# Output parts fetched three ahead of their split, and expert weight rows one per other part, in the stage after cross attention of a decoder layer

## The chip, the cores and the metric

One core of a Trainium2 chip. The metric is the device time of one execution in microseconds, the median over the runs shown; the profile is of one execution. PE is TensorE, DVE VectorE, ACT ScalarE, POOL GpSimd, SP SyncE, which issues most transfers. PEld is the weight load of PE.

## What is computed

A decoder layer on x of 16 x 100 tokens, width 512, fp32, with a context of 16 x 361 rows:

```python
x = layernorm(x + self_attention(x))            # 16 heads of 32, causal
x = layernorm(x + cross_attention(x, ctx))      # 16 query heads of 128, 4 key heads,
                                                # RMS norm on q and k, then o @ Wo (2048 x 512)
x = layernorm(x + ffn(x))                       # router over 8 experts, top 2, silu(x @ We + be),
                                                # weighted sum, projection, RMS norm
```

The 1600 tokens make NT = 13 tiles, twelve of 128 tokens and one of 64.

## The kernel before

Every fp32 product is made of three fast ones. `split` (L133) writes a high part (`dst.h`, a rounded copy, on ACT unless said otherwise, L137) and a low part (`dst.l`, source minus high, on DVE or POOL, L140). `mm3` (L145 to L147) multiplies high by high, high by low and low by high. So L137 and L140 are lines of a helper, and the names of the tiles tell the places apart.

The tile framework orders the instructions of each engine itself, by priority (program order, unless raised) along a timeline that it simulates. `in_turn` and `keep_in_program_order` add an order without a wait. Engines then run their queues in that order; SP too, whose transfers wait in its queue for what they need.

Stages around the change:

- Cross attention runs over 16 batches x 4 groups (b, g) of 4 heads. `x_scores` makes the scores, the row minimum on DVE (L746), the exponential on ACT (L757), the scaling on POOL (L759, tiles p2 and sums2); `x_turn` transposes the probabilities on PE into ptp (L767) and splits them; `x_attend` multiplies by the values, copies av out on ACT (L787) and stores it to the DRAM tiles od (L792).
- The output product (d_ functions) takes od back in parts. A part is (t, g): token tile t and group g, 128 x 4 x 128 values. `parts` lists the 52 of them: for tiles 0 to 9 tile by tile, and for the last TAIL = 3 tiles group by group. `d_load` fetches a part into `of` (2 buffers) and splits it into the pair `ot` (2 buffers), low on DVE for odd parts and on POOL for even ones. `d_part` multiplies it with the rows wo_g: 4 x 3 matmuls of 512 columns onto the tile's accumulator acc. After the fourth group `d_norm` adds x1d (L851, L852), normalises and stores x2d (L854).
- Parts 0 to 3 are written in the program among the last batch's groups (HEAD = 1 per group); the loop at L1320 handles the others, with part i + 1 loaded ahead of part i's product. The framework may run parts of the loop earlier, wherever PE would wait.
- The loop carries more: `d_turn` transposes a finished tile (L933), copies it on ACT (L940), adds a bias on POOL (L941) and stores xbd (L942); `d_logits` makes the router's logits (gb, L952, and lg on DVE, L956); `choose`, `settle` and `slots` work out on DVE, in many small operations (L1049 to L1224), which tokens go to which slot of which expert, ending in is_in (L1224), matmuls on gb (L1239) and idx (L1247). `settle(0, CUT)` needs the logits of tiles 0 to 8; the expert stage's first gathers (`e_gather`, L1263) need idx.
- `load_expert(e)` fetches an expert's four weight rows (128 x 512 each) into `f_e` (the pool stage, 3 buffers, L1312) and splits them into a slot of WH and WL, high on ACT and low on POOL, all four at one place. Experts 1, 2, 4, 5 come at tiles 2, 4, 6, 8; three more (wo_slot) each after the last tile's part of a group, when that group's rows of Wo are no longer needed, since they take their place; the last expert after the loop, two of its rows from the tile `raw`.

The expert stage (e_ functions) and the projection with two norms (f_ functions) follow.

On-chip pools are stacked from both sides. When a pool is opened over the place of a closed one, a tile waits for the tiles that it overlaps (`reuse_waits="tile"`). In a partition, d_in lies at bytes 159936 to 174272 (where attention's kv_in was), and on the other side c_3 (sums2, nm2) at 175232 to 175492, c_1 (nine buffers of p2) from 175520, both of cross attention; later d_3 (tiles x1 of `d_norm`) starts at 176544.

Of the kernel before, what the change touches and what calls it, by code (L numbers as in the profile page):

```python
# [9 lines left out]
FP = mybir.dt.float32  # L10
# [7 lines left out]
B, S, D = 16, 100, 512  # L18
T = B * S
KC = D // 128  # L20
# [4 lines left out]
NKV, HD2 = 4, 128  # L25
GR = NH // NKV
# [36 lines left out]
def tile_decoder_layer(  # L63
# [28 lines left out]
    nc = tc.nc  # L92
# [19 lines left out]
    def pair(p, shape, name, tag=None, bufs=None):  # L112
        k = {} if bufs is None else {"bufs": bufs}
        tag = tag or name
        return Pair(
            p.tile(shape, FR, name=f"{name}_h", tag=f"{tag}_h", **k),
            p.tile(shape, FR, name=f"{name}_l", tag=f"{tag}_l", **k),
        )

    def in_turn(ins, prev):  # L120

        if prev is not None:
            tc.add_manual_dep(
                ins.ins,
                prev.ins.name,
                mybir.DependencyInfo(
                    mybir.DependencyClass.NoSync, mybir.DependencyReason.DATA
                ),
                reason="in_turn",
            )  # L130
        return ins

    def split(dst, src, high=None, low=None):  # L133

        high, low = high or nc.scalar, low or nc.vector
        if high is nc.scalar:
            ins = nc.scalar.copy(dst.h, src)  # L137
        else:
            ins = high.tensor_copy(dst.h, src)  # L139
        low.tensor_tensor(dst.l, src, dst.h.bitcast(FP), ALU.subtract)  # L140
        return ins
# [70 lines left out]
    def kp(w):  # L212
        return w.rearrange("(k p) n -> p k n", p=128)

    NT = len(TT)
# [267 lines left out]
    def split_row(name, k):  # L483
        return split(units[name][:, k], ROW.pop((name, k)), nc.scalar, nc.gpsimd)
# [319 lines left out]
    for h in range(GR):  # L804
        x_scores(0, 0, h)
    order = [(b, g) for b in range(B) for g in range(NKV)]
    OT, X1 = {}, {}

    def d_open():
        kv_l.close()  # L810
        inp["d"] = pool(d_i, "d_in", 2)
# [2 lines left out]
    parts = [(t, g) for t in range(NT - TAIL) for g in range(NKV)]  # L814
    parts += [(t, g) for g in range(NKV) for t in range(NT - TAIL, NT)]

    def d_load(i):
        t, g = parts[i]
        n = TT[t][1]
        p = inp["d"]  # L820
        of = p.tile([128, GR, 128], FP, name=f"of_{t}_{g}", tag="of")
        nc.sync.dma_start(of[:, :, :n], od[t][:, g * GR : (g + 1) * GR, :n])
        OT[t, g] = pair(p, [128, GR, 128], f"ot_{t}_{g}", tag="ot")
        split(OT[t, g][:, :, :n], of[:, :, :n], low=nc.vector if i % 2 else nc.gpsimd)

    def d_part(i, among={}):

# [34 lines left out]
    for i, (b, g) in enumerate(order):  # L862
        if b == B - 1:
            if g == 0:
                d_open()
                d_load(0)
            for j in range(HEAD * g, HEAD * (g + 1)):
                d_load(j + 1)
                d_part(j)
                if parts[j][1] == NKV - 1:  # L870
                    d_norm(parts[j][0])
        if b + 1 < B:
            if g == 0:
                fetch_ctx(b + 1)
                split_ctx(b + 1, 0)
            if g < len(CH):
                kv_project(b + 1, g)
            if g + 1 < len(CH):
                split_ctx(b + 1, g + 1)
        if i + 2 < len(order):  # L880
            x_load(*order[i + 2])
        if b + 1 < B and g == NKV - 1:
            kv_turn(b + 1, 2)
        if b + 1 < B and 1 <= g < NKV - 1:
            kv_turn(b + 1, g - 1)
        nxt = order[i + 1] if i + 1 < len(order) else None
        for what in ("s0", "a-", "t0", "s1", "s2", "t1", "a0", "t2", "s3", "a1"):
            if what[0] == "s":
                if nxt:
                    x_scores(*nxt, int(what[1]))  # L890
            elif what[0] == "t":
                x_turn(b, g, int(what[1]))
            elif what[1] != "-":
                x_attend(b, g, int(what[1]))
            elif i:
                x_attend(*order[i - 1], 2)
        if i % 3 == 2 and 8 <= i < 8 + 3 * NKV * KC:
            w, k = divmod((i - 8) // 3, KC)
            load_row(f"wo_{w}", wo_slot[w], Wo4[w], k)
# [361 lines left out]
    def e_gather(i):  # L1261
        XG[i] = xsp.tile([128, D], FP, name=f"xs_{i}", tag="xs")
        nc.gpsimd.indirect_dma_start(  # L1263
            out=XG[i][:],
            out_offset=None,
            in_=x2d[: CUT * 128] if i < EARLY else x2d[:],
            in_offset=bass.IndirectOffsetOnAxis(ap=SLOT[i][0], axis=0),
        )
# [34 lines left out]

    raw = w1.tile([128, 2, D], FP, name="raw")

    def load_expert(e, last=False):
        for k in range(KC):
            if last and k > 1:
                f = raw[:, k - 2]
            else:  # L1310
                f = stage.tile([128, D], FP, name=f"f_e_{e}_{k}", tag="f")
                tc.keep_in_program_order(nc.sync.dma_start(f, kp(expert_w[e])[:, k]))  # L1312
            split(
                slot_of(e)[:, k],
                f,
                nc.vector if last and k == 1 else nc.scalar,
                nc.vector if last and k else nc.gpsimd,
            )

    for i in range(HEAD * NKV, len(parts)):  # L1320
        t, g = parts[i]
        if i + 1 < len(parts):
            d_load(i + 1)
        among = {}
        if t < NT - TAIL:
            if g == 1:
                d_turn(t - 1)
            if g == 3:
                among = d_logits(t - 1)
            if g == 0 and t in (2, 4, 6, 8):  # L1330
                load_expert(early[t // 2 - 1])
        elif t > NT - TAIL and g == 0:
            if t < NT - 1:
                d_turn(NT - TAIL - 1)
            else:
                among = d_logits(NT - TAIL - 1)
        elif (t, g) == (NT - 1, NKV - 1):
            d_turn(NT - TAIL)
        d_part(i, among)
        if g == NKV - 1:  # L1340
            with tc.high_priority(offset=URGENT if t >= NT - TAIL else 0):
                d_norm(t)
        if t == NT - 1 and g < NKV - 1:
            load_expert(wo_slot[g])
        if (t, g) == (CUT, 0):
            nc.sync.dma_start(raw, kp(expert_w[wo_slot[3]])[:, 2:])
        if t % 3 == 0 and t <= CUT and g == 3:
            choose(t - 3, t)
        if (t, g) == (NT - 1, 0):
            choose(CUT, CUT + 1)  # L1350
        if (t, g) == (CUT, 3):
            settle(0, CUT)
            slots(0, EARLY, CUT)
        if (t, g) == (NT - 1, 1):
            for k in range(4):
                e_gather(k)
    d_i.close()
    ck_l.close()
    load_expert(wo_slot[3], True)
    e_turn(0)  # L1360
    e_turn(1)
    e_product(0, d_logits(NT - TAIL))
# [412 lines left out]
```

## Time and profile before

| | us |
|---|---|
| median of 3 runs | 1432.21 (1428.25 to 1441.84) |
| the profiled execution | 1437.28 |
| its span, first to last instruction | 1435.6 |
| PE busy | 1342.1 (93%) |
| DVE, ACT, POOL busy | 954.1, 746.8, 731.1 |
| mean granted clock of PE | 0.973 of full |

How to read it: a matmul's duration in the profile overlaps the next one's, so pace is read from start to start (0.233 us for 512 columns at full clock). In the slices a digit is the busy share of 1/40 of the span, 35.9 us. In a timeline a line is start, duration, engine, source line, operation, output from input; in brackets how long the engine stood idle before it and what ended that. In a view by stretches the columns are from and to, length, busy time of PE, PEld, DVE, ACT and POOL with the number of instructions, the granted clock, the share of the transfer engines and GB/s.

The output product's first matmul starts at 1002.4 us, cross attention's last od store at about 1087, and the expert stage's first product at 1228.3.

### The profile page before, as it was taken

The numbers are of one execution on the slowest core, as the hardware profiler recorded it, in microseconds if no ns is written. First come the engines' busy times: TensorE is split into PE (matmuls) and PEld (weight loads), VectorE is DVE, ScalarE is ACT, GpSimd is POOL, SyncE is SP. The second block draws the span as 40 slices with busy tenths as digits, with TensorE's granted clock in tenths as the row PEclk, the third lists the DMA queues.
The fourth block names the chain that finished last, engine by engine and source line by source line (L and its number), as shares of the span: only waits on it lengthen the run. The fifth ranks groups of instructions, "written<-read, shape, count | busy, mean of one in ns | idle before, by whom it ended". The sixth has DMA issues, their size and how long they took to land. (4 is left out here: it accounts for less than half of the span.)

```text
span 1435.6 us, 25188 instructions
## 1 busy us (share of the span) xinstructions
PE 1342.1 (93%) x7952; PEld 1107.7 (77%) x7952; DVE 954.1 (66%) x2978; ACT 746.8 (52%) x1872; POOL 731.1 (51%) x854
## 2 busy tenths in 40 slices
PE   8999989999999999999999999999999897988884
PEld 6888878888778888888888888878887674666663
DVE  5766667775567777777777667767555559653698
ACT  4666643444436666566666566656553232332353
POOL 6877653443335555555555455545444445343542
PEclk9999999999999999999999999999999998899898
DMA  5221254555442232323233222223536554666674
GB/s 157 71 92 53 70 161 111 135 92 110 98 103 62 62 74 51 74 63 75 69 75 70 74 68 69 50 65 76 131 81 200 179 165 129 210 227 214 209 239 139
DMA packets 197873, 159.79 MB, mean 111 GB/s; under 512 B 133322, under 2 KB 152878, under 8 KB 197742
## 3 DMA queue, kind: packets, MB, share of 16 engines
q1 hardware_dynamic: 187904, 137.83, 36.2%
q0 software_dynamic: 4576, 14.95, 3.4%
q10 hardware_dynamic: 5262, 5.41, 1.3%
q8 instruction: 65, 1.06, 0.3%
q14 instruction: 66, 0.54, 0.1%
HBM read 107.16 MB, written 50.99 MB: 110 GB/s over the span
## 5 line engine op out<-in xcount | busy, mean ns | idle before, releaser
L759 POOL TENSOR_SCALAR p<-p,sums 100x361 f32<-100x361 f32 x256 | 146.4, 576 | 100.3 <-DVE sums L758 89.3
L746 DVE CUSTOM_DVE_ANT_0 p<-s,nmask 100x361 f32<-100x361 f32 x256 | 132.9, 527 | 64.7 <-PE s L147 56.2
L757 ACT ACTIVATE p<-p,nm 100x361 f32<-100x361 f32 x256 | 153.2, 602 | 39.8 <-DVE nm L746 36.5
L140 DVE TENSOR_TENSOR pT_l<-ptp,pT_h 128x400 fp32r<-128x400 f32 (+1 forms) x192 | 107.4, 567 | 59.3 <-ACT pT_h L137 58.8
L145 PE MATMUL pq<-WH 128*128 128x512 f32 (+2 forms) x272 | 106.5, 392 | 6.2 <-DVE WH L139 5.8
L767 PE MATMUL ptp<-ident,p 100*128 100x100 f32 (+1 forms) x768 | 107.6, 252 | 0.0
L140 POOL TENSOR_TENSOR cT_l<-cf,cT_h 128x512 fp32r<-128x512 f32 (+1 forms) x48 | 54.4, 1134 | 104.2 <-ACT cT_h L137 102.3
L137 ACT CAST pT_h<-ptp 128x400 fp32r<-128x400 f32 (+1 forms) x192 | 91.3, 487 | 30.2 <-PE ptp L767 29.7
L767 PEld LDWEIGHTS ptp<-ident,p 100*128 100x128 f32 (+1 forms) x768 | 95.6, 152 | 13.5 <-POOL p L759 2.3
L146 PE MATMUL pq<-WL,WH 128*128 128x512 f32 (+2 forms) x272 | 104.1, 383 | 0.0
L147 PE MATMUL pq<-WH,WL 128*128 128x512 f32 (+2 forms) x272 | 103.8, 382 | 0.0
L147 PE MATMUL acc<-WH,ot_l 128*128 128x512 f32 (+1 forms) x208 | 87.3, 421 | 8.7 <-DVE ot_l L140 6.9
L145 PE MATMUL acc<-WH,ot_h 128*128 128x512 f32 (+1 forms) x208 | 87.2, 419 | 5.5 <-ACT ot_h L137 5.5
L145 PE MATMUL s<-kT_h,WH 128*100 128x362 f32 x256 | 88.5, 356 | 2.4 <-ACT kT_h L137 2.4
L145 PE MATMUL av<-pT_h,WH 128*128 128x400 f32 (+1 forms) x192 | 77.1, 401 | 11.6 <-ACT pT_h L137 11.1
L146 PE MATMUL acc<-WL,ot_h 128*128 128x512 f32 (+1 forms) x208 | 85.1, 409 | 0.0
L147 PE MATMUL s<-kT_h,WL 128*100 128x362 f32 x256 | 84.5, 330 | 0.0
L146 PE MATMUL s<-kT_l,WH 128*100 128x362 f32 x256 | 83.9, 328 | 0.0
L614 POOL TENSOR_TENSOR qs<-qs,r_q 128x512 f32<-128x512 f32 (+1 forms) x52 | 54.0, 1068 | 58.0 <-DVE r_q L169 47.5
L140 POOL TENSOR_TENSOR WL<-qf,WH 128x400 fp32r<-128x400 f32 x64 | 67.3, 1051 | 31.0 <-ACT WH L137 27.7
L145 PE MATMUL pv<-WH,cT_h 128*128 128x512 f32 (+1 forms) x192 | 80.0, 417 | 1.3 <-DVE WL L140 1.3
L145 PE MATMUL pk<-WH,cT_h 128*128 128x512 f32 (+1 forms) x192 | 77.7, 405 | 0.2
(330 smaller groups left out, 4030.0 us busy)
## 6 DMA issues: line engine op xcount, KB each, us to landing
qf<-qd SPq DMA_DIRECT2D x64, 200.0 KB
of<-od SPq DMA_DIRECT2D x48, 256.0 KB
cf<-in_ctxT SPq DMA_DIRECT2D x16, 722.0 KB
eb<-in_expert_b SPq DMA_DIRECT2D x32, 256.0 KB
ysd<-xs SPq DMA_DIRECT2D x32, 256.0 KB
f_e<-in_expert_w SPq DMA_DIRECT2D x30, 256.0 KB
f_wq<-in_Wq SPq DMA_DIRECT2D x16, 256.0 KB
f_wo<-in_Wo SPq DMA_DIRECT2D x16, 256.0 KB
```

Source lines behind the costliest of these rows:

```text
L137: ins = nc.scalar.copy(dst.h, src)
L140: low.tensor_tensor(dst.l, src, dst.h.bitcast(FP), ALU.subtract)
L145: nc.tensor.matmul(out, a.h, b.h, start=start, stop=False)
L146: nc.tensor.matmul(out, a.h, b.l, start=False, stop=False)
L147: nc.tensor.matmul(out, a.l, b.h, start=False, stop=stop)
L614: nc.gpsimd.tensor_tensor(qr[:, hs, :], qr[:, hs, :], rs[:n, hs].unsqueeze(2).to_broadcast([n, GR, HD2]), ALU.mult,)
L746: nc.vector.tensor_tensor_reduce(out=p, in0=sc[:, :SE], in1=nmask, scale=1.0, scalar=BIG, op0=ALU.add, op1=ALU.min, accum_out=nm,)
L757: nc.scalar.activation(p, p, AF.Exp, bias=nm, scale=-1.0, accum_out=sh)
L759: nc.gpsimd.tensor_scalar(p, p, sh, 1.0, ALU.mult, ALU.mult)
L767: nc.tensor.transpose(pt[:n, h, :], probs[h][:, c0 : c0 + n], ident[:S, :S])
```

## The change

- `d_load` is cut in two. `d_fetch(i)` takes an `of` tile and starts the transfer; `d_load(i)` splits it. In the loop, `d_fetch` runs up to part i + 3 before `d_load(i + 1)`. A pool d_in2 with one buffer of 128 x 4 x 128 (2048 bytes a partition) is opened ahead of the loop; every third part from part 5 on takes its `of` there, the others in d_in. While attention is going on (parts 0 to 4) there is one fetch ahead of one split as before.
- Expert rows are fetched two ahead of the row that is next to be split (`e_fetch`), and split one at a time in `e_rows(i)`: the sixteen rows of experts 1, 2, 4, 5 at parts 6, 8, ... 36, then those of the first three wo_slot experts from part 43 on, with the four rows of an expert on three parts, and the first two rows of the last expert fetched there and split after the loop (`load_last`). Each row's high part is ordered on ACT behind the high part of the output part that was split last.

```diff
-    OT, X1 = {}, {}
+    OT, OF, X1 = {}, {}, {}
+    split_last = [None]
...
+    def d_fetch(i):
+        t, g = parts[i]
+        n = TT[t][1]
+        p = inp["d2"] if "d2" in inp and i % 3 == 2 else inp["d"]
+        OF[i] = of = p.tile([128, GR, 128], FP, name=f"of_{t}_{g}", tag="of")
+        nc.sync.dma_start(of[:, :, :n], od[t][:, g * GR : (g + 1) * GR, :n])
+
     def d_load(i):
         t, g = parts[i]
         n = TT[t][1]
-        p = inp["d"]
-        of = p.tile([128, GR, 128], FP, name=f"of_{t}_{g}", tag="of")
-        nc.sync.dma_start(of[:, :, :n], od[t][:, g * GR : (g + 1) * GR, :n])
-        OT[t, g] = pair(p, [128, GR, 128], f"ot_{t}_{g}", tag="ot")
-        split(OT[t, g][:, :, :n], of[:, :, :n], low=nc.vector if i % 2 else nc.gpsimd)
+        of = OF.pop(i)
+        OT[t, g] = pair(inp["d"], [128, GR, 128], f"ot_{t}_{g}", tag="ot")
+        split_last[0] = split(
+            OT[t, g][:, :, :n], of[:, :, :n], low=nc.vector if i % 2 else nc.gpsimd
+        )
...
                 d_open()
+                d_fetch(0)
                 d_load(0)
             for j in range(HEAD * g, HEAD * (g + 1)):
+                d_fetch(j + 1)
                 d_load(j + 1)
                 d_part(j)
...
-    def load_expert(e, last=False):
+    def load_last(e):
         for k in range(KC):
-            if last and k > 1:
+            if k > 1:
                 f = raw[:, k - 2]
             else:
-                f = stage.tile([128, D], FP, name=f"f_e_{e}_{k}", tag="f")
-                tc.keep_in_program_order(nc.sync.dma_start(f, kp(expert_w[e])[:, k]))
+                f = ROW.pop((f"e_{e}", k))
             split(
                 slot_of(e)[:, k],
                 f,
-                nc.vector if last and k == 1 else nc.scalar,
-                nc.vector if last and k else nc.gpsimd,
-            )
-
+                nc.vector if k == 1 else nc.scalar,
+                nc.vector if k else nc.gpsimd,
+            )
+
+    BY = (NT - TAIL) * NKV
+    erows = [(e, k) for e in early for k in range(KC)]
+    split_at = [HEAD * NKV + 2 + 2 * r for r in range(len(erows))]
+    for g in range(NKV - 1):
+        first = BY + TAIL * (g + 1)
+        erows += [(wo_slot[g], k) for k in range(KC)]
+        split_at += [first + min(k, TAIL - 1) for k in range(KC)]
+    erows += [(wo_slot[-1], k) for k in range(2)]
+    split_at += [len(parts)] * 2
+    rows_in, rows_out = [0], [0]
+
+    def e_rows(i):
+        while rows_out[0] < len(erows) and split_at[rows_out[0]] <= i:
+            e, k = erows[rows_out[0]]
+            in_turn(split_row(f"e_{e}", k), split_last[0])
+            rows_out[0] += 1
+            e_fetch()
+
+    def e_fetch():
+        while rows_in[0] < min(rows_out[0] + 2, len(erows)):
+            e, k = erows[rows_in[0]]
+            fetch_row(f"e_{e}", e, kp(expert_w[e]), k)
+            rows_in[0] += 1
+
+    d2 = ExitStack()
+    inp["d2"] = pool(d2, "d_in2", 1)
+    begun = HEAD * NKV + 1
+    e_fetch()
     for i in range(HEAD * NKV, len(parts)):
         t, g = parts[i]
+        while begun < min(i + 4, len(parts)):
+            d_fetch(begun)
+            begun += 1
         if i + 1 < len(parts):
             d_load(i + 1)
+        e_rows(i)
         among = {}
...
-            if g == 0 and t in (2, 4, 6, 8):
-                load_expert(early[t // 2 - 1])
...
-        if t == NT - 1 and g < NKV - 1:
-            load_expert(wo_slot[g])
...
+    d2.close()
     d_i.close()
     ck_l.close()
-    load_expert(wo_slot[3], True)
+    load_last(wo_slot[3])
```

`fetch_row` and `split_row` are helpers that were there: the first starts a row's transfer into the pool stage, the second splits it, high on ACT and low on POOL.

More of the change, by code (lines that the diff above doesn't have):

```diff
@@ L1315, in load_expert @@
                 f,
-                nc.vector if last and k == 1 else nc.scalar,
-                nc.vector if last and k else nc.gpsimd,
-            )
+                nc.vector if k == 1 else nc.scalar,
+                nc.vector if k else nc.gpsimd,
+            )
+    BY = (NT - TAIL) * NKV
+    erows = [(e, k) for e in early for k in range(KC)]
+    split_at = [HEAD * NKV + 2 + 2 * r for r in range(len(erows))]
+    assert split_at[-1] < BY + TAIL
+    for g in range(NKV - 1):
[20 more added lines that the diff above has]
+    e_fetch()
     for i in range(HEAD * NKV, len(parts)):
         t, g = parts[i]
+        while begun < min(i + 4, len(parts)):
+            d_fetch(begun)
+            begun += 1
         if i + 1 < len(parts):
             d_load(i + 1)
+        e_rows(i)
         among = {}
```

## The prediction

> **What bounds the kernel now.** I read the page's busy shares and slices first, then the busy time in ten-microsecond stretches around the output product that follows cross attention, then the waits there, and last the timelines of PE, ACT, DVE, POOL and SP.
>
> ```profile
> PE 1342.1 (93%) x7952; PEld 1107.7 (77%) x7952; DVE 954.1 (66%) x2978; ACT 746.8 (52%) x1872; POOL 731.1 (51%) x854
> PE   8999989999999999999999999999999897988884
> PEclk9999999999999999999999999999999998899898
> ```
>
> PE is the bound nearly everywhere; its nines break after slice 31 (about 1110 us), which is where the change works. By stretches (PE, PEld, DVE, ACT, POOL busy, then the granted clock):
>
> ```profile
> 1110.00:1120.00 10.00, 5.89 (x27) 3.88 (x25) 5.64 (x16) 2.69 (x5) 3.99 (x4) 1.00 0.59 192
> 1120.00:1130.00 10.00, 9.09 (x38) 7.29 (x39) 7.54 (x23) 2.54 (x6) 6.54 (x5) 0.83 0.52 160
> 1190.00:1200.00 10.00, 6.36 (x22) 3.79 (x21) 9.90 (x25) 2.74 (x5) 4.64 (x4) 0.83 0.53 163
> 1210.00:1220.00 10.00, 4.80 (x47) 3.03 (x46) 9.05 (x24) 2.28 (x6) 5.44 (x5) 0.79 0.33 83
> ```
>
> A hole in PE is followed by a lower clock. The waits of PE from 1095 to 1230 us (us, times, longest) name the splits of the output parts, then routing:
>
> ```profile
> PE acc L147 <- DVE ot_l L140: 5.6, 4, 3.6
> PE acc L145 <- ACT ot_h L137: 5.5, 4, 3.2
> PE gb L1239 <- DVE is_in L1224: 5.0, 2, 4.3
> ```
>
> The largest hole, on the timelines of PE and ACT:
>
> ```profile
> 1119.06 0.50 PE L145 MATMUL acc<-WH,ot_h 128*128 128x512 f32 x1 [3.17 <-ACT ot_h L137]
> 1116.54 0.62 ACT L137 CAST WH<-f_e 128x512 fp32r<-128x512 f32 x1 [6.12 <-DMA f_e<-in_expert_w]
> 1118.39 0.61 ACT L137 CAST ot_h<-of 128x512 fp32r<-128x512 f32 x1
> ```
>
> ACT works in order: two expert-row copies, waiting for their transfers, stood ahead of the part's copy that PE needed. The same view has ACT waiting 28.0 us for of over twelve times; most of that is inside PE's slack.
>
> The end of the stage has another limit, the routing chain on DVE, from the logits of tile 8 (1175.04) to is_in (1216.89): 41.9 us. Its small operations stretch while POOL runs:
>
> ```profile
> 1183.55 3.82 POOL L140 TENSOR_TENSOR WL<-f_e,WH 128x512 fp32r<-128x512 f32 x3
> 1184.83 1.29 DVE L1033 TENSOR_SCALAR i_full<-i_full 128x8 int32<-128x8 int32 x1
> 1187.32 0.19 DVE L1033 TENSOR_SCALAR i_had<-i_had 128x80 int32<-128x80 int32 x1
> ```
>
> The same line takes 1.29 us on 8 columns and 0.19 on 80.
>
> **What the Trainium skill says.** "TensorE: Matmul & The Clock Gate", Part 1, has PE's clock halve after an idle window of about 3.4 us and return after about as much work. The trace agrees in size: from 1120.44 to 1123.60, seven acc matmuls start 0.45 us apart against 0.233 before, 1.5 us lost; but 1.0 us of holes at 1149–1151 was enough for the next such stretch. The same page's section on the array ("Architectural detail") calls ACT and DVE strict FIFO, as the three lines on ACT's queue show. "SBUF — State Buffer", section "SBUF: two separate sides", has DVE and POOL share a port pair as an exclusive lock held for a whole instruction; the two L1033 lines fit. No page gives the transfer's latency for this load; I take the trace's.
>
> **The change part by part.** Counts stay: 52 loads of of, 30 of f_e, the same splits. Only places, one buffer and issue orders are new. I count PE time up to the logits of tile 8, then the chain, then the rest.
>
> *Stalls removed.* PE holes on ot_h or ot_l before 1175: 1.30 (at 1042.6), 1.79 (1086.7), 0.74, 3.17, 0.65, 0.37, 0.59, sum 8.6 us. Slow stretches behind three of them (1089.5, 1120.4, 1151.1): 1.4 + 1.5 + 1.5 = 4.4. Together 13.0. With a fetch issued as soon as a third buffer falls free, about two parts (2 x 12 x 0.233 = 5.6 us) ahead, against a landing of 4.2 us (issue at 1088.46, copy at 1092.63), transfers no longer decide; a row's copy (0.62) and low half (1.29) stand behind a part's copy, one per two parts, not four at once.
>
> *Stalls that stay.* The split pairs still have two buffers: part i+1 may be split only when i-1 has been multiplied, and needs 0.62 + 1.29 + about 0.2 of the 2.8 us; one d_turn addition on POOL (1.29) uses that slack up. DVE can also stand before an ot_l: at 1106.40 it had waited 5.43 us for an x1d load, which no part of the change hurries. SP is in order too, and the earlier fetches stand ahead of x1d loads and xbd stores, waiting for a split. I take 3 us (1 to 6).
>
> *Filler lost.* This is the price I see in the new pool. d_in ends at byte 174272 of a partition; d_in2 takes the next 2048, where cross attention has all its sums2 and nm2 (175232 on) and the first p2 buffer (175520), whose last tenant is the first head of the last group. Part 5, the first in d_in2, can be loaded only after that head's last transpose, and parts 6, 7 and all later ones queue behind it through accumulators and pairs. The trace shows such a wait already: the x1d loads, whose tiles lie on p2 too, go out with the last ptp:
>
> ```profile
> 1076.92 0.53 PE L767 MATMUL ptp<-ident,p 100*105 100x100 f32 x4
> 1077.20 1.37 SPq L851 DMA_DIRECT2D x<-x1d  x3
> ```
>
> Before, some 190 acc matmuls (16 parts) were interleaved with attention by 1077; then only parts 0 to 4 can be. Eleven parts, 31 us of PE work, move behind attention, which finishes earlier by as much if PE stays full without them. From 1057.7 to 1064.2 it did, on attention alone. The drain of the last group can't: last score to last p takes 3.1 us (1063.56 to 1066.7), transposes, splits (0.49 + 0.57) and av another 5, with 3.6 us of PE work in these 8. The load of part 5 starts some 5.8 us after the last score, lands 4.2 later, is copied in 0.6: PE restarts at about 10.5, so 6.9 idle, less what is left of part 4 (0 to 2.8), plus 1.5 of slow clock. I take 6 (2 to 11). Sum to the logits: -13 + 3 + 6 = -4.
>
> *The chain.* The fourth early expert's rows sat on POOL from 1183.6 to 1189.9, inside the chain; five DVE operations took 5.9 us there where 0.2 each is usual. These rows now end with part 36, before part 39's logits. From part 43 on as many wo-slot rows fall in as before, 12. I take -3 (0 to -6).
>
> *After the chain.* PE still had 21 acc matmuls to do behind is_in (1218.0 to 1225.3), twelve at the slow pace (2.4 us lost). If earlier tail parts let them run ahead of the slot matmuls, expert work starts that much sooner; but PE's order may keep them behind. The tail's own holes (1.77, 3.64) and the rest go into the wait for is_in, so they count nothing. I take -1.5 (0 to -5). The expert stage after it is PE-bound (10.00 of 10 busy from 1345 to 1375), so the shift carries through. Loading the last expert's first two rows early gains nothing: their copy at 1223.40 waited for PE.
>
> Sum: -4 - 3 - 1.5 = -8.5 us. The profiled execution took 1437.28 us (span 1435.6 and 1.7 around it), so 1428.8 there; it lies 5.1 above the median of the runs, 1432.2, for which I get 1423.7.
>
> **The rivals.** (a) *All of it pays*: drain covered by part 4 (2), stalls down to 1, chain -6, rest -5: -21, 1411. For: ACT's 28 us of waiting for of; against: two pairs. (b) *It cancels*: stalls 6, drain 11: -0.5, 1432. (c) *Attention starves*: with filler, its groups came 13.4 us apart (copies of av from 1004.44 to 1058.13) for some 4.6 us of PE work each. If that pace is its own and not the filler's, four groups leave 35 us idle less 14 for five parts, 21, with the drain 28, with four slow stretches 34: -13 + 3 + 34 - 4.5 = +19.5, 1452. It is slower than before once this loss passes 14.5 us. Against: the full stretch at 1057.7.
>
> **How the numbers follow.** The forecast has 0.42 (own range 1416 to 1430), (a) 0.36, (b) 0.08, (c) 0.14. One per cent, 14.3 us, is about what a measurement of this kernel can tell from no change. So faster 0.38, within 0.48, slower 0.14. From 1404 to 1444 both unknown prices are covered, and the better part of (c) and a little below (a) is left out.
>
> **What would show it.** Right: no acc wait over 1 us on ACT ot_h after attention; no burst of four WH<-f_e; the last od store some 30 us earlier; of_1_1's load right behind the last ptp, a PE hole of 4 to 7 us there; the stretch from lg to is_in under 40 us. Wrong: parts of tiles 1 to 3 still interleaved with attention (then no loss), or PE holes before the last ptp above 14 us in sum (then c), or the acc waits as long as now.

## Result and profile after: slower by 0.4%

The kernel after took 1439.34 us, median of 20 runs (1432.62 to 1448.74), beside 1433.59 for 20 runs of the kernel before (1428.25 to 1441.84): ratio 1.0038 [1.0023, 1.0053]. A second comparison gave 1.0040 [1.0022, 1.0059]. So it is slower by 5 to 6 us, which is under 1%, but not the 8.5 us gain of the forecast.

The page of the kernel after:

```profile
PE 1341.8 (93%) x7952; PEld 1105.7 (77%) x7952; DVE 951.5 (66%) x2978; ACT 746.9 (52%) x1872; POOL 732.7 (51%) x854
...
PE   8999989999999999999999999999979997789984
...
PEclk9999999999999999999999999999999998789997
```

PE does the same work, with its breaks in other places: one 7 in slice 30 (behind attention), and 77 in slices 34 and 35, the end of the stage. The waits of PE from 1095 to 1230 us, the view in which four holes on ot_h and four on ot_l stood before:

```profile
PE acc L147 <- DVE ot_l L140: 5.6, 1, 5.6
PE pte L1284 <- DMA xs<-x2d,idx: 5.2, 2, 3.1
PE gb L1249 <- DVE is_in L1234: 5.2, 1, 5.2
```

From 1095 us on no part waits for its high half any more; the waits for low halves come to the same sum in one piece. New is the second line: PE waits for the gathers of the expert stage. What the fetch was meant for works, too. The waits of ACT from 1050 to 1175, of before and then of after:

```profile
ACT ot_h L137 <- DMA of<-od: 22.3, 10, 4.3
```

```profile
ACT ot_h L137 <- PE acc L146: 52.6, 32, 3.0
...
ACT ot_h L137 <- DMA of<-od: 4.5, 1, 4.5
```

ACT now waits for PE, not for transfers. The price of d_in2 is there as well: the first load into it goes out behind the last ptp, and PE stops, then works at a lower clock (SP's timeline, then PE's, then ten us by stretches):

```profile
1048.31 0.99 SPq L480 DMA_DIRECT2D f_e<-in_expert_w  x2
1049.40 0.37 SPq L823 DMA_DIRECT2D of<-od  x1
```

```profile
1047.46 0.53 PE L767 MATMUL ptp<-ident,p 100*105 100x100 f32 x4
...
1055.65 0.80 PE L145 MATMUL acc<-WH,ot_h 128*128 128x512 f32 x1 [5.85 <-ACT ot_h L137]
```

```profile
1050.00:1060.00 10.00, 4.35 (x13) 3.47 (x14) 1.62 (x11) 1.57 (x3) 2.47 (x8) 0.66 0.94 193
```

The loss lies further on. A table of the stations from tile 8's logits (lg) to the first expert product, one row for each profiled execution; "chain" is from lg to the end of the second is_in, "rows" the expert rows that POOL splits in it, all of them rows of the late experts, the last column the first product (first ph matmul) less idx:

| kernel | ratio to before [interval] | lg of tile 8 | chain (rows) | is_in to idx | idx | product 0 less idx |
|---|---|---|---|---|---|---|
| before | | 1175.0 | 41.9 (12) | 1.5 | 1218.3 | 10.0 |
| before2 | | 1175.3 | 42.6 (12) | 1.5 | 1219.3 | 10.3 |
| after | 1.0038 [1.0023, 1.0053] | 1170.0 | 42.7 (11) | 5.0 | 1217.6 | 16.2 |
| after2 | 1.0040 [1.0022, 1.0059] | 1172.8 | 40.3 (9) | 4.9 | 1218.0 | 16.3 |
| nolap | 1.0054 [1.0034, 1.0073] | 1170.5 | 40.5 (9) | 4.7 | 1215.8 | 16.5 |
| fe_act | 1.0032 [1.0017, 1.0048] | 1173.8 | 42.7 (11) | 4.0 | 1220.5 | 9.9 |
| nolap_act | 1.0012 [0.9998, 1.0026] | 1170.4 | 42.7 (11) | 5.1 | 1218.2 | 9.3 |
| nolap_act_j | 1.0014 [0.9994, 1.0035] | 1172.2 | 40.2 (9) | 5.0 | 1217.4 | 8.8 |
| early_only | 1.0003 [0.9990, 1.0017] | 1172.9 | 42.6 (12) | 3.9 | 1219.4 | 10.1 |
| nolap_early | 1.0032 [1.0018, 1.0045] | 1168.8 | 42.7 (12) | 3.9 | 1215.4 | 9.6 |
| fetch_only | 1.0146 [1.0123, 1.0168] | 1190.3 | 43.1 (12) | 3.4 | 1236.8 | 9.5 |
| rows_only | 1.0070 [1.0045, 1.0095] | 1176.5 | 40.8 (10) | 5.2 | 1222.4 | 15.7 |
| tail_pool_j | 1.0025 [1.0010, 1.0040] | 1172.6 | 41.8 (11) | 1.2 | 1215.7 | 14.0 |
| no_wl | one run | 1170.2 | 29.3 (0) | 4.0 | 1203.4 | 16.3 |
| dve_low | 0.9986 [0.9967, 1.0005] | 1175.7 | 47.6 (1) | 1.2 | 1224.5 | 9.3 |
| after_dve_low | 0.9990 [0.9973, 1.0008] | 1169.9 | 43.3 (0) | 3.2 | 1216.3 | 9.3 |
| before_dve_low | 0.9993 [0.9978, 1.0008] | 1172.3 | 46.2 (1) | 1.2 | 1219.7 | 8.8 |
| dve_idx_ra | 0.9961 [0.9946, 0.9977] | 1171.4 | 38.3 (1) | 1.2 | 1210.9 | 13.0 |
| before_idx | 0.9978 [0.9962, 0.9994] | 1169.5 | 39.1 (1) | 1.2 | 1209.8 | 11.5 |

The median of the kernel before lay between 1429.33 and 1433.59 us in the comparisons, so kernels are compared by their ratios. In before and before2 product 0 starts at 1228.3 and 1229.5, in after and after2 at 1233.8 and 1234.3: later by 5.2 us in the mean, as much as the time grew.

The delay does not last, though. The fifth product starts at 1253.2 and 1253.1 in before and before2, and at 1252.0 and 1251.2 in after and after2; the ninth at 1268.0 and 1268.1, and at 1267.5 and 1267.6. By then PE has made the delay good. idx is worked out twice, first for eleven products and then for the other 21, and the kernel after falls behind again where the second is needed (DVE's timeline of before2 and then of after):

```profile
1272.04 0.18 DVE L1247 CAST idx<-gb 128x21 int32<-128x21 f32 x1 [0.24 <-PE gb L1239]
```

```profile
1277.09 0.18 DVE L1257 CAST idx<-gb 128x21 int32<-128x21 f32 x1 [0.22 <-PE gb L1249]
```

The thirteenth product starts at 1287.4 and 1286.3 in the two executions of before, and at 1293.9 and 1294.6 in those of after. The second idx needs the logits of the last tiles, and the last of these came at 1244.2 and 1245.5, and at 1252.7 and 1251.9. So the late first product equals the loss in size, but it is not shown to be the way in which the time is lost.

### The profile page after: what moved, and what is told of

It is laid out like the page before. It is cut to its first block, busy times and chain, and to the rows that moved or that the text cites. A ratio compares the mean times of both kernels' runs of the same rounds, so it can differ in the third digit from the quotient of the medians.

```text
span 1437.2 us, 25178 instructions
## 1 busy us (share of the span) xinstructions
PE 1341.8 (93%) x7952; PEld 1105.7 (77%) x7952; DVE 951.5 (66%) x2978; ACT 746.9 (52%) x1872; POOL 732.7 (51%) x854
## 5 line engine op out<-in xcount | busy, mean ns | idle before, releaser
L145 PE MATMUL av<-pT_h,WH 128*128 128x400 f32 (+1 forms) x192 | 77.1, 402 | 10.6 <-ACT pT_h L137 10.3
```

The lines of the kernel that those rows point to most:

```text
L145: nc.tensor.matmul(out, a.h, b.h, start=start, stop=False)
```

## The experiments

**Which readings belong to the kernel** (before2 and after2 are the two kernels unchanged).

> The kernel before, profiled once more, to tell which of its readings belong to the kernel and which to one execution. If the expert stage simply carries its start through to the end, the 5.6 us hole of PE at 1330 (a gather's semaphore) should not come back, the first expert product should stand near 1228 and the span near 1430.5, the median less 1.7. If the hole belongs to the kernel, it is there again within 1 us of its size, the span is near 1435, and the late first product of the kernel after (5.5 us) was paid for by something else.

Span 1429.7 us, product 0 at 1229.5, no hole at 1330. The hole belonged to one execution, and so did most of the 5.1 us by which the profiled execution lay above the median.

> The kernel after once more. If the late rows belong to the kernel, product 0 again follows idx by 15 to 17 us, idx follows the end of is_in by 4 to 5 us, and the logits of tile 8 stand at 1168 to 1174; ratio to the kernel before 1.002 to 1.006. If they belong to one execution, product 0 follows idx by 10 us.

All as expected: idx 4.9 behind is_in, product 0 another 16.3 behind idx.

**Why product 0 is late.** SP's timeline of the kernel after and then of the kernel before (f_e are expert rows, x2d the stores of normalised tiles):

```profile
1200.19 4.84 SPq L480 DMA_DIRECT2D f_e<-in_expert_w  x3
1218.80 0.34 SPq L862 DMA_DIRECT2D x2d<-x  x1
1219.35 0.27 SPq L480 DMA_DIRECT2D f_e<-in_expert_w  x1
...
1220.22 0.42 SPq L862 DMA_DIRECT2D x2d<-x  x1
1220.85 0.88 SPq L480 DMA_DIRECT2D f_e<-in_expert_w  x2
```

```profile
1209.35 2.82 SPq L1312 DMA_DIRECT2D f_e<-in_expert_w  x3
1221.23 0.34 SPq L854 DMA_DIRECT2D x2d<-x  x1
```

In the kernel after the last three fetches come two rows ahead of their split, that is late in the program, and in SP's queue they stand behind a load that waits for idx (L1301) and behind the stores of tiles 10 and 11, which wait for their norms. They go out ten us later than before, and their copies follow at 1224.97 and 1229.53 on ACT and at 1233.28 on DVE; product 0 starts at 1233.84. The rows are not all that product 0 had to wait for. Right ahead of it PE stands at the transposes of tile 12, which need that tile's norm, and DVE's copy of the last row stands in its queue behind the same norm (PE's timeline of the kernel after):

```profile
1233.23 0.66 PE L943 MATMUL ptx<-ident,x 64*128 64x64 f32 x4 [3.66 <-DVE hit L1064]
1233.84 1.20 PE L145 MATMUL ph<-WH,xsT_h 128*128 x2
```

This wait of 3.66 us stands ahead of product 0 in the five executions in which it comes some 16 us behind idx (after, after2, nolap, rows_only and no_wl), and in no other. Whether the rows, the norm or PE's order held product 0 was not separated.

A product picks its expert's rows by a register, so it waits for every row of WH and WL. Three edits test this. fe_act issues the last three rows from ACT's queue; nolap keeps d_in2 away from attention; nolap_act does both (of fe_act only the choice of the queue is shown):

```diff
-            fetch_row(f"e_{e}", e, kp(expert_w[e]), k)
+            q = nc.scalar if len(erows) - rows_in[0] <= 3 else nc.sync
+            fetch_row(f"e_{e}", e, kp(expert_w[e]), k, q)
...
```

```diff
-        p = inp["d2"] if "d2" in inp and i % 3 == 2 else inp["d"]
+        p = inp["d2"] if "d2" in inp and i % 3 == 2 and i >= 20 else inp["d"]
```

> The kernel after, with the last three weight rows (one of expert 0, two of expert 6) issued from ACT's queue, so that they no longer stand behind the stores of x2d on SP. Theory B (late rows): their copies stand before 1223, product 0 starts at 1227 to 1229 instead of 1233.8, time 4 to 6 us under the kernel after, about 1434. Theory A (filler lost, rows without effect): product 0 is held by the gathers and the slow clock, at 1231 or later, time within 1.5 us of the kernel after. Theory C (the expert stage absorbs its start): product 0 earlier by 5, time within 1 us of the kernel after.

> The kernel after, with d_in2 used from part 20 on only: the parts before part 20 keep the two buffers of d_in, which don't overlap attention's tiles, so parts can fill attention again. Theory A (filler was lost): some 180 acc matmuls interleaved with attention again, no 5.9 us hole behind the last ptp and no slow stretch there, less whatever stalls come back for want of a third buffer in parts 5 to 19 (up to 4 us); logits of tile 8 at 1165 to 1168 instead of 1170.0, time 3 to 5 us under the kernel after, 1434 to 1436. Theory B (the late rows of the last expert alone set the start of the expert products): these hang on the norm of tile 10, which moves with the logits, so the gain carries through here too; the delay between the last slot matmul and product 0 stays at 16 us. Theory C (the expert stage absorbs its start): logits earlier, time within 1 us of the kernel after, 1439.

> Both edits together: d_in2 from part 20 on, the last three rows from ACT's queue. If both losses are real and separate (A and B): product 0 at 1221 to 1225, time 8 to 10 us under the kernel after, 1429 to 1431, that is 2 to 4 us faster than the kernel before. If only one of them counts, 1434. Under theory C 1439.

The delay behaved as theory B says: 9.9 and 9.3 us behind idx with the edit, 16.5 without it. The time did so for one pair: nolap_act is 4.2 per mille (6 us) under nolap, though only 2.6 to 2.8 per mille (4 us) under the kernel after, where both theories together had 8 to 10. fe_act is only 0.6 to 0.8 per mille under the kernel after, far from the 4 to 6 us expected. Its fetches moved into another queue that works in order (ACT's timeline of fe_act):

```profile
1214.28 0.34 ACTq L480 DMA_DIRECT2D f_e<-in_expert_w  x1
1218.53 0.20 ACT L157 ACTIVATE a_ln<-v_ln 128x1 f32<-128x1 f32 x1 [5.09 <-DVE v_ln L179]
1218.64 0.60 ACT L137 CAST WH<-f_e 128x512 fp32r<-128x512 f32 x1
1218.77 0.34 ACTq L480 DMA_DIRECT2D f_e<-in_expert_w  x1
```

The last row now waits behind a norm's logarithm. In this execution idx, too, came 2.5 to 2.9 us later than in the two of the kernel after. Yet product 0 came 3.4 to 3.9 us earlier than there, and the time gained only 1 us, so an earlier product 0 is not an equal gain. The second idx came at 1276.0 and the thirteenth product at 1294.0, about as in the kernel after.

Theory A failed: nolap's logits were no earlier than those of the kernel after, and its time no better. Over the pairs the overlap has no steady sign (nolap over after by 1.5 per mille, nolap_act under fe_act by 2.0, nolap_early over early_only by 2.9).

early_only is the cleanest test: the kernel after with the late rows as in the kernel before (the lists of late rows go, `load_expert` comes back).

```diff
+        if t == NT - 1 and g < NKV - 1:
+            load_expert(wo_slot[g])
...
-    load_last(wo_slot[3])
+    load_expert(wo_slot[3], True)
```

> The kernel after, with the rows of the last four experts fetched and split as in the kernel before (four at a time behind the last tile's parts), the first sixteen rows still one per other part, and the fetch three ahead. Theory B (late rows): the last fetches stand ahead of bat's load and the x2d stores on SP again, product 0 follows idx by 10 us instead of 16.2, time 4 to 6 us under the kernel after, 0.999 to 1.001 of the kernel before. Rival (the delay comes from the gathers or from the slow clock): product 0 at idx plus 14 or more, time within 1.5 us of the kernel after.

```profile
1203.36 8.62 SPq L1322 DMA_DIRECT2D f_e<-in_expert_w  x6
1220.53 0.34 SPq L862 DMA_DIRECT2D x2d<-x  x1
```

All fetches ahead of the first x2d store again, product 0 10.1 us behind idx, and the time equal to that of the kernel before, 3.5 per mille (5 us) under the kernel after. So in this pair the late rows are all of the loss, and the rest of the change comes to nothing. The other pairs with and without late rows go the same way by other amounts: fe_act lies 0.6 to 0.8 per mille under the kernel after, nolap_act 4.2 and nolap_early 2.2 under nolap; for early_only and nolap_act the intervals are apart. That the late rows cost time is shown, somewhere from 1 to 6 us. By which way is not: in early_only's profiled execution, 2.8 us above the median of its runs, the second idx (1275.8) and the thirteenth product (1292.5), too, came 4 to 6 us later than in before and before2. Why the rest comes to nothing is the second question.

> As early_only (last four experts' rows as in the kernel before), and d_in2 used from part 20 on only. This tells what the overlap of d_in2 with attention's tiles costs when the late rows are out of the way. If parts that fill attention again are worth the 5 us hole with its slow stretch: 4 us under early_only, 0.997 to 0.998 of the kernel before. If the time is given back ahead of tile 8's logits by stalls of parts 5 to 19: within 1.5 us of early_only.

It was slower than early_only, which neither expectation allows for. Its profiled execution, 4.3 us under the median of its runs, shows nothing that would explain it (logits at 1168.8, product 0 at 1224.9); this stays open. It also means that an edit of one line can move the time by 2.9 per mille in a way that none of the theories has, so a single pair proves little.

**What each half does alone.** fetch_only has the old load_expert in every place; rows_only has no d_in2 and fetches a part right ahead of its split.

> Only the fetch three ahead, with d_in2; all expert rows as in the kernel before. Theory A (what the stage gains in front of tile 8's logits comes from the third buffer): logits of tile 8 at 1170 to 1172 as in the kernel after. Rival (it comes from spreading the rows): the burst of row copies stalls the parts' copies again, holes of 3 us on ACT ot_h as at 1116 in the kernel before, plus the 5.9 us hole behind attention: logits of tile 8 at 1176 to 1180, time 1.002 to 1.004 of the kernel before.

> Only the spread rows; a part's fetch one ahead of its split, no d_in2. If the spreading brings the gain ahead of tile 8's logits: 1170 to 1172 there; if the third buffer does: 1174 to 1176. Theory B holds in both cases that product 0 follows idx by 15 us or more, so that the time is 1.003 to 1.006 of the kernel before.

Each half alone has the larger ratio (1.0146 and 1.0070 against 1.0038 and 1.0040 for both together); of rows_only the interval still meets those of the kernel after. In fetch_only the logits came at 1190.3, past even the rival's range, by a way that I had not named. PE's waits from 1050 to 1175, and ACT's timeline:

```profile
PE ptx L943 <- DVE x L181: 11.5, 4, 3.5
```

```profile
1099.12 0.20 ACT L157 ACTIVATE a_ln<-v_ln 128x1 f32<-128x1 f32 x1 [1.95 <-DVE v_ln L179]
1101.41 0.62 ACT L137 CAST WH<-f_e 128x512 fp32r<-128x512 f32 x1 [2.09 <-DMA f_e<-in_expert_w]
1101.94 0.20 ACT L158 ACTIVATE y_ln<-a_ln 128x1 f32<-128x1 f32 x1
```

The parts' fetches, now far ahead, push a burst of row fetches back in SP's queue; ACT stands at the burst's first copy with a norm half done, between a_ln and y_ln, and PE waits for that norm's tile: four holes of 2.6 to 3.5 us. The burst's wait had moved from the parts to the norms. In rows_only ACT still waits 23.2 us for of:

```profile
ACT ot_h L137 <- DMA of<-od: 23.2, 7, 6.3
```

**PE's order behind is_in.** In the kernel after one slot matmul starts and then twelve of the tail's matmuls stand between it and the others:

```profile
1211.80 0.17 PE L1249 MATMUL gb<-is_in,named 128*128 128x11 f16 x1 [5.17 <-DVE is_in L1234]
1211.82 0.77 PE L147 MATMUL acc<-WH,ot_l 128*128 128x512 f32 x1
...
1216.44 0.58 PE L1249 MATMUL gb<-is_in,named 128*128 128x11 f16 x17
```

nolap_act_j takes the second choice first, so that no slot matmul is ready before all are:

```diff
-        todo = [(j, t) for t in range(upto) for j in range(2)]
+        todo = [(j, t) for t in range(upto) for j in (1, 0)]
```

> As nolap_act (d_in2 from part 20 on, the last three rows issued from ACT), and the slot matmuls take the second choice before the first, so that none of them is ready before both halves of is_in are: ten acc matmuls of tile 11 then stand ahead of the slot matmuls in PE's queue instead of behind the first of them. Theory D (PE's order costs 3.5 us between is_in and idx, and the first gathers, idx plus 10 us, set the start of the expert products): idx 1.5 to 2 us behind is_in instead of 5.0, product 0 at 1223 to 1225 instead of 1227.5, time 3 us under nolap_act. Rival (the gathers' own latency or the second routing sets the expert stage): idx earlier, time within 1 us of nolap_act. Second rival: tile 11's low half isn't there in time and is_in waits behind it, idx no earlier.

The second rival came true. The tail's matmuls now stand ahead of the slot matmuls, and one of them waits for a low half that stands in DVE's queue inside the chain:

```profile
1208.56 0.50 PE L147 MATMUL acc<-WH,ot_l 128*128 128x512 f32 x1 [3.45 <-DVE ot_l L140]
...
1215.80 0.61 PE L1249 MATMUL gb<-is_in,named 128*128 128x11 f16 x18
```

Those behind it ran at the slow clock until 1212.2, so idx was again 5.0 us behind is_in. tail_pool_j moves these low halves to POOL, on early_only, with the same order:

```diff
-            OT[t, g][:, :, :n], of[:, :, :n], low=nc.vector if i % 2 else nc.gpsimd
+            OT[t, g][:, :, :n], of[:, :, :n], low=nc.vector if i % 2 and i < 40 else nc.gpsimd
```

> As early_only, with the low halves of the last three tiles' odd parts on POOL instead of DVE, and the slot matmuls behind both halves of is_in. If PE's tail holes (5.6 and 3 to 5 us on DVE ot_l) delay is_in's matmuls through PE's order, and DVE's own chain gets 4 us shorter without six of these splits: idx 1.5 us behind is_in, chain from the logits of tile 8 to is_in 38 us, time 3 to 6 us under early_only, 0.996 to 0.998 of the kernel before. If POOL's longer work stretches DVE's small operations instead, the chain stays at 42 us or grows to 46, time equal to early_only or up to 4 us over it.

idx came 1.2 us behind is_in, as expected, and the chain was no shorter (41.8), as the rival has it: six splits less on DVE, six more on POOL, and 2.2 per mille over early_only.

**What POOL costs the chain.** no_wl leaves the low halves of three late experts' rows out, so that its output is less exact:

```diff
-            in_turn(split_row(f"e_{e}", k), split_last[0])
+            if e in wo_slot:
+                ins = nc.scalar.copy(slot_of(e).h[:, k], ROW.pop((f"e_{e}", k)))
+            else:
+                ins = split_row(f"e_{e}", k)
+            in_turn(ins, split_last[0])
```

> The kernel after without the low halves (on POOL) of the rows of three late experts (3, 7, 0), left out to see what they cost the routing chain: its output is less exact. If POOL's rows stretch DVE's small operations, the chain from the logits of tile 8 to the end of is_in falls from 42.7 to 34 to 37 us (some 0.6 us for each of the 11 rows). If the chain has another reason, it stays at 41 to 43.

The chain fell to 29.3 us, further than expected: 13.4 us for 11 rows of 1.29 us, beside after; beside after2 it is 11.0 for 9, again 1.2 for a row. The same operations on DVE, of after and then of no_wl:

```profile
1184.55 4.49 DVE L1136 TENSOR_SCALAR named<-seq,lo,token 128x128 f16<-128x128 f32 x6
...
1203.44 6.59 DVE L1217 TENSOR_TENSOR last<-last,opn 128x8 f32<-128x8 f32 x7
```

```profile
1182.65 1.62 DVE L1136 TENSOR_SCALAR named<-seq,lo,token 128x128 f16<-128x128 f32 x6
...
1194.78 1.36 DVE L1217 TENSOR_TENSOR last<-last,opn 128x8 f32<-128x8 f32 x7
```

Six and seven operations take 2.8 and 4.8 times as long beside POOL. The one run took 1422.75 us, 6.6 under the median of the kernel before, with the late rows still in it.

**The low halves on DVE.** A row takes DVE 0.69 us, less than POOL's row costs the chain (13.4 / 11 = 1.2). The edit is one word, on three kernels (for early_only and for the kernel before in load_expert):

```diff
+            low = nc.vector if e in wo_slot else nc.gpsimd
```

> As early_only, with the low halves of the last experts' rows (13 on POOL before, 3 on DVE already) all on DVE. In the kernel without those low halves the chain was 29.3 us against 42.7 for 11 rows, so a row on POOL costs the chain some 1.2 us, twice the 0.65 that DVE needs to do it itself. Theory E (the routing chain, stretched by POOL, bounds the stage from tile 8's logits on): chain 34 to 38 us, product 0 at 1222 to 1226, time 4 to 7 us under early_only, 0.995 to 0.997 of the kernel before. Rival F (DVE works in order, and a row whose transfer or high copy is late holds the chain up): chain 41 us or more, DVE waiting for WH inside it, time equal to early_only or over it.

> The kernel after with the low halves of the rows of experts 3, 7, 0 and 6 on DVE. The rows come one per part here, so DVE should wait for them less than in dve_low; the late fetches stay, unless the shorter queue of POOL lets them go. Theory E: chain 34 to 37 us; with the late rows product 0 still 14 us or more behind idx, time 3 to 6 us under the kernel after, 0.999 to 1.001 of the kernel before; if the fetches go early now, 0.995 to 0.997. Rival F: chain 41 or more, time as the kernel after.

> The kernel before with the same one edit: the last experts' low halves on DVE. It tells whether the change of this study matters for what the edit brings. Theory E: the fourth early expert's four rows stay on POOL inside the chain, so the chain falls from 42 to 36 to 39 us and the time by 3 to 6 us, 0.996 to 0.998. If spreading the rows was needed for it, dve_low lies 3 us or more under this one; if the change is worth nothing here, the two are equal.

Rival F was right on the chain (43 to 48 us), theory E on the time for one kernel only: after_dve_low is 5 per mille (7 us) under the kernel after, the other two 1.7 and 0.7 per mille better than their bases. Here before_dve_low shows another thing: POOL has no expert row left between these two, so the rows at 1183.6 in the kernel before were not those of an early expert (POOL's timeline):

```profile
1151.62 1.38 POOL L140 TENSOR_TENSOR WL<-f_e,WH 128x512 fp32r<-128x512 f32 x1 [0.98 <-ACT WH L137]
...
1208.98 1.30 POOL L140 TENSOR_TENSOR WL<-f_e,WH 128x512 fp32r<-128x512 f32 x1 [5.07 <-ACT WH L137]
```

In after_dve_low DVE waits little; it is full. The last norms have moved into the chain (DVE's timeline):

```profile
1202.93 0.68 DVE L860 TENSOR_TENSOR x<-acc,x 128x512 f32<-128x512 f32 x1
...
1206.04 1.28 DVE L140 TENSOR_TENSOR WL<-raw,WH 128x512 fp32r<-128x512 f32 x2
1207.24 0.68 DVE L175 BATCH_NORM_STATS2 st_ln<-x 64x6 f32<-64x512 f32 x1
```

Its gain goes with something else: as the norms are early, the x2d stores are early on SP (1206 and 1210), the rows behind them no longer late (product 0 9.3 behind idx), and the second idx comes at 1265.5 instead of 1277.1.

**The chain first.** dve_idx_ra and before_idx order the norms of the last three tiles and the last expert's late rows on DVE behind the first idx (chain_end is its last companion, bat; in dve_idx_ra the last three fetches also go to ACT):

```diff
-        nc.vector.tensor_tensor(x2[:n], acc[:n], x2[:n], ALU.add)
+        ins = nc.vector.tensor_tensor(x2[:n], acc[:n], x2[:n], ALU.add)
+        if t >= NT - TAIL:
+            in_turn(ins, chain_end[0])
...
```

> As after_dve_low, and three things ordered on DVE behind the first idx and its two companions: the norms of the last three tiles and the low halves of the last expert's last three rows; the last three fetches from ACT's queue. In after_dve_low these norms and rows took 10 us of DVE inside the chain, DVE being busy without a break from 1178 to 1213. Theory E (the chain is the bound): chain 32 to 36 us instead of 43.3, idx at 1204 to 1208 instead of 1216.3, product 0 at 1214 to 1219, time 4 to 8 us under after_dve_low, 0.993 to 0.996 of the kernel before. Rival G (the expert stage is bound by the last tiles' logits and the second idx, which these norms precede): product 0 earlier, but the second idx no earlier than 1265 and the time within 1.5 us of after_dve_low.

> The kernel before with the same two edits on DVE (late rows' low halves on DVE; the last norms and rows behind the first idx), its fetches as they were. If theory E holds, it gains 4 to 8 us on the kernel before too (0.994 to 0.997); what dve_idx_ra lies under it is then what the change of this study is worth once its gain isn't lost in the chain: 5 us if all of the gain ahead of tile 8's logits comes through, 0 if rival G holds.

```profile
1209.27 0.46 DVE L1238 TENSOR_TENSOR is_in<-seq,tile_of 128x288 f16<-128x288 f32 x1
1210.91 0.17 DVE L1261 CAST idx<-gb 128x11 int32<-128x11 f32 x1 [1.19 <-PE gb L1253]
...
1211.15 1.86 DVE L862 TENSOR_TENSOR x<-acc,x 128x512 f32<-128x512 f32 x3
```

The chain fell to 38.3 and 39.1 us, less than expected, but both kernels are now faster than the kernel before: 0.9961 [0.9946, 0.9977] and 0.9978 [0.9962, 0.9994]. dve_idx_ra is the fastest of the kernels that leave nothing out. Theory E holds in direction: a shorter chain goes with a shorter time, though product 0 at 1223.9 and 1221.2, 5 and 7.7 us earlier than in the mean of before and before2, brought 5.6 and 3.2 us. Product 0 gained only 1.8 us on after_dve_low (1223.9), since PE, in order, waits for tile 10's norm ahead of the gathers' transposes:

```profile
1219.60 1.08 PE L947 MATMUL ptx<-ident,x 128*128 128x128 f32 x4 [6.46 <-DVE r_ln L170]
```

Between the two lie 1.7 per mille (2.4 us), for the change of this study and the other queue of three fetches together; their intervals overlap, so this is not settled.

## Why the prediction was wrong, step by step

*Stalls removed, -13, stalls that stay, +3, filler lost, +6: -4 to the logits.* The mechanisms were right, one by one: the waits for of went (22.3 to 4.5 us), parts 0 to 4 alone lay inside attention (60 acc matmuls ahead of the last ptp, 185 before), attention ended earlier by 29 us (last ptp 1047.46 against 1076.92), and the hole behind it was 5.85 and 4.9 us in two executions. The first pair of profiles even gave -5.1, by luck. Four profiled executions with before's order up to this point put the logits at 1173.0 in the mean (1169.5 to 1175.3), and nine with after's order at 1172.1 (1169.9 to 1175.7): -0.9. From 1020 to 1180 the four lost 10.3 us in holes of PE and 3.0 in slow clock (from the granted clock per ten us), and all of that is gone: from 1100 to 1180 the nine have no hole and no slow clock. But between 1020 and 1100 they have 9.0 us of holes, about what the forecast had for the hole and the stalls that stay, and 5.5 us of slow clock (3.4 to 6.8). The term that was mis-sized is this slow clock behind attention, for which filler lost held 1.5; what of it fell inside the hole cost nothing. "TensorE: Matmul & The Clock Gate", Part 1, of the Trainium skill has the clock halved by an idle window of about 3.4 us until a busy one has passed, so that one slow stretch should cost 1.7 us (an estimate from the page, half of 3.4); the losses here, 1.7 to 6.8 us, are all multiples of 1.7. How many such stretches there are differs by the execution, which one profile can't say.

*The chain, -3.* This step rested on lines that were misread. The rows on POOL from 1183.6 to 1189.9 were not the fourth early expert's. The sixteen early rows start on POOL at 1033.7 to 1154.4 in the kernel before; those at 1183.6 are the next four, the first late expert's, and before_dve_low, which moves late rows alone, has none there. So nothing that the change takes away lay in the chain. It held 12 late rows before, in both executions, and 11 and 9 after, since the late rows now begin at part 43. Two executions each: 41.9 and 42.6 us before, 42.7 and 40.3 after, -0.7 in the mean. The price of a row was too low, if anything (1.2 us by no_wl, 0.75 in the forecast). "SBUF — State Buffer", section "SBUF: two separate sides", has DVE and POOL lock each other out for whole instructions; no_wl fits that and gives it a price, 1.2 us for a row, but no run here tells the lock from another cause of the stretching.

*After the chain, -1.5.* This is the step that failed in sign: product 0 came 9.6 us later behind is_in than before, not 1.5 earlier. It failed in three places. I had the 21 acc matmuls behind is_in as work in the way of the expert stage. They were cover: the gathers need about ten us from idx to the second transpose (1217.62 to 1227.58 in the kernel after), and PE now waits 2.09 and 3.13 us for them. Then the slot matmuls were split by twelve others, +3.5 from is_in to idx, where I had expected PE's order to help or to do nothing. And "loading the last expert's first two rows early gains nothing" considered the copy's wait for PE, not the queue that the fetch would stand in. These fetches were moved past two stores and a load on SP that wait for norms and for idx, and product 0 came 16.2 us behind idx instead of 10.0. I had named SP's order for the earlier fetches (x1d, xbd) and not for the last ones. With the late rows put back (early_only) the 16.2 are 10.1 again and the time is that of the kernel before; but how the loss gets from there to the end stays open.

*The sum.* The stations add up to product 0: logits -3.8 (both pairs), chain -0.7, is_in to idx +3.5, idx to product 0 +6.1, in all +5.1, beside a measured 0.38%, 5.4 us. That they agree is luck. The -3.8 is -0.9 over more executions, and "the shift carries through" did not hold: the kernel after had made up the 5.1 by the fifth product and lost time again behind the second idx. From product 0 to the end of the span the nineteen executions took from 196.6 to 207.2 us.

*The rivals.* (b), it cancels, is what is left when the late rows are mended (early_only, 1.0003), though not by its own numbers (+4 to the logits, -4.5 behind them). (c), attention starving, didn't occur: PE was full on attention alone, and the one hole of 5.85 us lay behind it. (a) counted on -5 behind the chain, where the loss was. None of the rivals had a loss behind the chain, and the one on the slower side lay in attention.

*What would show it.* Seen as written: no acc wait on ACT ot_h over 1 us after the first part, no bursts of four rows, the od stores 36 us earlier (last av copy 1085.77 to 1049.84), of_1_1 right behind the last ptp, a hole of 4 to 7 us. Missed: the stretch from lg to is_in under 40 us. That list ended at is_in; nothing in it followed the fetches, the second idx or the products behind it.

## What to carry to other kernels

When transfers are moved later, walk through the queue that issues them and ask what each neighbour in front waits for; a fetch behind a store that waits for a result goes out as late as that result, ten us later here. Before a late start is called the loss, follow it through the next stations: these 5 us at the first product were made good four products on, and the time went elsewhere. Matmuls in front of a gather's result may be its cover and not its delay. And where a serial chain of small DVE operations bounds a stage, try first to take the wide operations of POOL and of DVE itself out of it: that made both kernels faster, by 2 to 4 per mille, which no overlap ahead of the chain did here. And read which rows, tiles or parts a line stands for by counting them from the start: the name alone did not tell an early expert's rows from a late one's.

## What the runs showed of the hardware

A tensor-tensor operation of 128 x 512 on POOL (1.29 us) made a chain of DVE operations about 1.2 us longer (13.4 us for 11 of them), nearly its own length and almost twice the 0.69 that DVE needs for the same operation; the forecast had 0.75 for a row. The slow clock between 1020 and 1180 us cost 1.7 to 5.1 us in four executions of before's order and 3.4 to 6.8 in nine of after's, each a multiple of 1.7 us.
